# Two chained attentions on one core: held sums, halves added by ones products, a busy TensorE at the head

## The chip, the cores and the metric

The kernel runs on one core of a Trainium2 chip. The metric is the device time of one execution in microseconds (us). A core has TensorE for matrix products (PE in the profile; PEld is its weight load), VectorE (DVE), ScalarE (ACT), GpSimd (POOL) and SyncE (SP), which here issues transfers.

## The reference, cut to what matters

Eight images of 64 channels and 64 x 64 points (4096 tokens) pass two attention layers, all in fp32. Layer 0 has keys of 8 channels; layer 1 normalizes in groups first and has keys of 64 channels.

```python
# layer 0, per image
f = einsum('oc,bcn->bon', Wf, xf) + bf          # 8 x 4096
g = einsum('oc,bcn->bon', Wg, xf) + bg          # 8 x 4096
hh = einsum('oc,bcn->bon', Wh, xf) + bh         # 64 x 4096
beta = softmax(einsum('bci,bcj->bij', f, g), axis=2)
x = x + einsum('bcj,bij->bci', hh, beta)
# layer 1, per image
xn = group_norm(x, gamma, beta)                  # 8 groups of 8 channels
q, k, v = split(einsum('oc,bchw->bohw', w_qkv, xn) + b_qkv)
attn = softmax((q @ k) * 64**-0.5)
x = x + einsum('oc,bchw->bohw', w_proj, attn @ v) + b_proj
```

## The kernel before

An image's 4096 tokens lie in two halves of 64 partitions each. Each half of the queries is cut in four chunks of 512 columns (NC = 4, CW = 512), the keys in 16 tiles (NT = 16) of 2 x 128 tokens. Per tile TensorE makes scores, ScalarE makes their exponentials `e` (128 x 2048), TensorE weighs the values with them into an accumulator, and DVE adds the tile's exponentials into `esum`, from which the softmax denominators come. Six buffers hold exponentials: one is free again when it has been weighed and added.

The layers run in the order: layer 0 of image 0, layer 0 of image 1, layer 1 of image 0, layer 0 of image 2, layer 1 of image 1, and so on.

The adding, and the two ways by which a finished chunk gets its denominators:

```python
ppool = ctx.enter_context(tc.tile_pool(name="ppool", bufs=6))     # the exponentials "e"
...
at.weigh(acc, e[:, p], t, p, j == 0, j == 2 * NT - 1, cols)        # TensorE
...
added = vector.tensor_add(esum, first if t == 1 else esum, e).ins  # DVE, 128 x 2048
...
def halves():
    if other is not None:
        vector.tensor_add(raw, raw, other)
    vector.tensor_add(esum[:, 0], esum[:, 0], esum[:, 1])          # 128 x 1024

def transposed():            # one way: DVE adds over partitions by transposing, then 4 DMAs
    vector.tensor_reduce(part, esum[:, 0].rearrange("p h (i b) -> p b (h i)", b=32),
                         axis=AX.X, op=ALU.add, apply_transpose=True)
    ...
def sums(spare):             # the other: TensorE adds over partitions by products with ones
    for h in range(2):
        for i in range(2):
            row = 32 * (2 * h + i)
            matmul(z[row : row + 32, 0:width], ones[:, 0:32], esum[:, 0, h, ts(i, width)],
                   start=True, stop=True, tile_position=(0, row))
    nc.scalar.copy(zs, z[:, 0:width])
    ...                      # 4 DMAs to zt
def reciprocals(): ...       # reciprocal, one DMA out, two broadcasting DMAs back into r
def result():
    vector.tensor_mul(raw, raw, r)
    self.residual(raw, c)    # layer 0: raw + bias + x, and statistics for layer 1
```

Which way is taken, and when. A held chunk keeps its sums in a buffer that is free for the time, and its halves are added when layer 1 has begun:

```python
held = at.holds(c)
if at.kind == 1 or next_kind == 1 or held:
    when = now + 4
    if at.kind == 0:
        when = (i // NC + 1) * NC * NT + 1 + 3 * c       # in the layer 1 that follows
    for s, u in ((0, halves), (1, transposed), (5, reciprocals), (8, result)):
        at_step(when + s, behind(u), 0)
    return
behind(halves)()
at_step(now + delay, lambda: sums(spare), BANK)
at_step(now + delay + 4, behind(reciprocals), 0)
at_step(now + delay + 8, behind(result), 0)
...
def holds(self, c):
    return self.kind == 0 and self.b > 0 and c < (1 if self.b == 1 else NC - 1)
def home(self, c):                                        # where held sums lie
    if self.b > 1:
        if c == 0:
            layers1[self.b].own(F32)
        return layers1[self.b].parts[:, c, :]
    layers0[2].own_vt()
    return layers0[2].vt.rearrange("q p t c -> q (p t c)")
```

So all four chunks of image 0 and chunks 1 and 2 of image 1 go by `sums`, the others by `transposed`.

The start of image 0: the first 512 columns are projected straight to their places (`project_direct`), the rest by `project`, whose results are spread by DMAs. Both write to a buffer `full` of which there is one.

```python
def project_direct(self):
    full = work.tile([P, 2, CW], F32, tag="full", bufs=1, name="full_direct")
    high = work.tile([P, 2, CW], F32R, tag="high", bufs=1, name="high_direct")
    for i, dst in enumerate((self.f, self.g)):
        matmul(ps[:, i, :], direct[:, i, :], x_tiles[self.b][:, 0:CW], start=True, stop=True)
        nc.scalar.activation(full[:, i, :], ps[:, i, :], AF.Identity, bias=bias2[:, i : i + 1])
        vector.tensor_copy(high[:, i, :], full[:, i, :])
        vector.scalar_tensor_tensor(dst[:, 0:CW], high[:, i, :].bitcast(F32),
                                    lowmask2[:, i : i + 1], full[:, i, :], ...)
...
copy = vector.tensor_copy if self.kind == self.b == c == 0 else nc.scalar.copy   # values
...
for i in range(4):                                        # Newton steps for 1/sqrt(variance)
    vector.scalar_tensor_tensor(w, y, y, ve, op0=ALU.mult, op1=ALU.mult)
    vector.tensor_scalar(w, w, -0.5, 1.5, op0=ALU.mult, op1=ALU.add)
    vector.tensor_mul(y, y, w)
```

`matmul` and, where `tight` is set, `vector` keep their instructions in the order of the program; elsewhere a scheduler orders them.

Of the kernel before, what the change touches and what calls it, by code (L numbers as in the profile page):

```python
# [9 lines left out]
F32 = mybir.dt.float32  # L10
# [9 lines left out]
CW = 512  # L20
P = 128
# [47 lines left out]
def fast_path(  # L69
# [19 lines left out]
    nc = tc.nc  # L89
    B, C, N = x.shape  # L90
    C8 = WfT.shape[1]
    NH = N // 2
    NC = NH // CW
# [4 lines left out]
    const = ctx.enter_context(tc.tile_pool(name="const", bufs=1))  # L98
    xpool = ctx.enter_context(tc.tile_pool(name="xpool", bufs=3))
    proj = ctx.enter_context(tc.tile_pool(name="proj", bufs=1))  # L100
# [20 lines left out]

    made_last = {}
    added = None
    tight = False

    def in_order(made, engine="tensor"):

# [20 lines left out]
    vector = InOrder()  # L148

    def matmul(*args, **kwargs):  # L150
        in_order(nc.tensor.matmul(*args, **kwargs))  # L151

    def behind(work_):


        def made():
            with tc.issue_after(added):
                work_()

        return made  # L160
# [22 lines left out]
        return t  # L183


    w1 = const.tile([P, 2, C8], F32, name="w1")
    for i, (w, queue) in enumerate(((WfT, nc.scalar), (WgT, nc.sync))):
        for h in range(2):
# [24 lines left out]
    with tc.issue_after(masked):  # L213
# [10 lines left out]
        wfg = const.tile([P, 2, 4, C8], F32, name="wfg")  # L224
        nc.vector.tensor_copy(wfg, w1.unsqueeze(2).broadcast_to([P, 2, 4, C8]))
    wfg = wfg.rearrange("p i s c -> p (i s c)")
    fgb_low = const.tile([P, 2], F32, name="fgb_low")
    fgb, lowmask = fgb_low[:, 0:1], fgb_low[:, 1:2]
    for j in range(2):
# [20 lines left out]
    nc.vector.tensor_single_scalar(odd, lane, 1, op=ALU.bitwise_and)  # L250
    lowmask32 = const.tile([P, 1], F32, name="lowmask32")
    nc.vector.tensor_scalar(lowmask32, odd, -1.0, None, op0=ALU.mult)
    ones = const.tile([P, C], F32, name="ones")
    nc.vector.memset(ones, 1.0)


    QP = 2 * CW // P
# [67 lines left out]
    class Attention:  # L325
# [7 lines left out]

        def holds(self, c):

            return self.kind == 0 and self.b > 0 and c < (1 if self.b == 1 else NC - 1)

        def values(self, src, w, c):

            ps = pair()  # L340
            for t in range(TPC):
                for m in range(2):
                    for h in range(2):
                        matmul(
                            ps[ts(m, C), h, ts(t, C)], src[ts(h, C), ds(t * P + m * C, C)],
                            w[ts(h, C), :], start=True, stop=True,
                        )

            copy = vector.tensor_copy if self.kind == self.b == c == 0 else nc.scalar.copy
            copy(  # L350
                self.vt[:, :, ts(c, TPC), :],
                ps[:, :, 0 : TPC * C].rearrange("k p (t c) -> k p t c", c=C),
            )

        def finish(self, acc, esum, c, index):

            n = f"{self.name}_{c}"
            raw = work.tile([P, CW], F32, tag="raw", bufs=4, name=f"raw_{n}")
            other = self.total(raw, acc, index)
            zt = small.tile([P, QP], F32, tag="zt", bufs=4, name=f"zt_{n}")  # L360
            width = CW // 2
            r = four = None
# [4 lines that stand above are left out]
                vector.tensor_add(esum[:, 0], esum[:, 0], esum[:, 1])  # L367

            def transposed():


                nonlocal four
                both_ = work.tile([P, 8 * QP], F32, tag="zs", name=f"part_{n}")
                part = both_[:, 0:32]
                four = both_[:, 32:].rearrange("p (a k) -> p a k", k=QP)
                vector.tensor_reduce(
                    part, esum[:, 0].rearrange("p h (i b) -> p b (h i)", b=32),
                    axis=AX.X, op=ALU.add, apply_transpose=True,
                )
                for a in range(4):  # L380
                    nc.sync.dma_start(four[:, a, :], part[ts(a, 32), :])

            def sums(spare):

                z = banks[:, spare, :]

                zs = work.tile([P, width], F32, tag="zs", name=f"zs_{n}")
                for h in range(2):
                    for i in range(2):
                        row = 32 * (2 * h + i)  # L390
                        matmul(
                            z[row : row + 32, 0:width], ones[:, 0:32], esum[:, 0, h, ts(i, width)],
                            start=True, stop=True, tile_position=(0, row),
                        )
                nc.scalar.copy(zs, z[:, 0:width])
                for h in range(2):
                    for i in range(2):
                        row = 32 * (2 * h + i)
                        nc.sync.dma_start(zt[row : row + 32, :], zs[row : row + 1, :])  # L399

            def broadcast():
                nonlocal r
                r = work.tile([P, CW], F32, tag="r", name=f"r_{n}")

            def reciprocals():
                rt = stash[:, ts(index, QP)]
                if four is not None:
                    vector.tensor_reduce(
                        zt, four.rearrange("p a k -> p k a"), axis=AX.X, op=ALU.add
                    )  # L410
                vector.reciprocal(rt, zt)
                broadcast()
                dealt = recips[index]
                nc.sync.dma_start(dealt, rt)
                for h in range(2):
                    row = dealt[ts(h, C), :].rearrange("p e -> (p e)")
                    nc.sync.dma_start(r[ts(h, C), :], row.partition_broadcast(C))

            def result():
                vector.tensor_mul(raw, raw, r)  # L420
                self.residual(raw, c)

            return halves, transposed, sums, reciprocals, result
# [52 lines left out]
    class Layer0(Attention):  # L476
# [4 lines left out]
        def before(self):  # L481

            def begin():
                if self.b == 1:
                    self.own(F32R)
                else:
                    self.parts = proj.tile([P, 2, NH], F32R, tag="fg", name=f"fg_{self.name}")
                    if self.b != 2:  # L490
                        self.own_vt()
                self.f, self.g = self.parts[:, 0, :], self.parts[:, 1, :]
                self.st = small.tile(
                    [P, NC, nc.vector.BN_STATS_DIM], F32, tag="st", name=f"st_{self.name}"
                )
                if self.b > 0:
                    self.project_all()
                else:
                    self.project_direct()
                    self.project(0, (1,))  # L500

            def rest():
                self.project(1)
                with tc.issue_after(self.sent.ins):
                    for b in (1, 2):
                        load_x(b)

            if self.b == 0:
                return [(-1, begin, True), (0, rest, True)] + [
                    (  # L510
                        (-1, 1, 5, 8)[c],
                        lambda c=c: self.values(x_tiles[0][:, ts(c, CW)], wh, c),
                        True,
                    )
                    for c in range(NC)
                ]

            s, spread = (28, 32) if self.b == 1 else (0, 28)  # L520
            return [(s, begin, True), (spread, self.spread, False)] + [
                (
                    (36, 38, 43, 45)[c],
                    lambda c=c: self.values(x_tiles[self.b][:, ts(c, CW)], wh, c),
                    True,
                )
                for c in range(NC)
            ]
# [4 lines left out]
        def home(self, c):  # L533

            if self.b > 1:
                if c == 0:
                    layers1[self.b].own(F32)
                return layers1[self.b].parts[:, c, :]
            layers0[2].own_vt()
            return layers0[2].vt.rearrange("q p t c -> q (p t c)")  # L540

        def project_direct(self):

            ps = pair()
            full = work.tile([P, 2, CW], F32, tag="full", bufs=1, name="full_direct")
            high = work.tile([P, 2, CW], F32R, tag="high", bufs=1, name="high_direct")
            for i, dst in enumerate((self.f, self.g)):
                matmul(
# [110 lines left out]
    class Layer1(Attention):  # L659
# [8 lines left out]
        def before(self):  # L668
# [32 lines left out]
            def deviations():  # L701
# [8 lines left out]
                )  # L710
                y = guess.bitcast(F32)
                w = small.tile([P, 1], F32, tag="w", name=f"w_{n}")
                for i in range(4):
                    vector.scalar_tensor_tensor(w, y, y, ve, op0=ALU.mult, op1=ALU.mult)
                    vector.tensor_scalar(w, w, -0.5, 1.5, op0=ALU.mult, op1=ALU.add)
                    vector.tensor_mul(y, y, w)
# [179 lines left out]
    def finished(i, now):  # L896
# [7 lines left out]
        if at.kind == 1 or next_kind == 1 or held:  # L904
# [4 lines left out]
            for s, u in ((0, halves), (1, transposed), (5, reciprocals), (8, result)):  # L909
                at_step(when + s, behind(u), 0)  # L910
            return
        behind(halves)()

        spare = outer[c % 2 if at.kind == 0 else 1]
        delay = 7 if at.kind == 0 else 5
# [34 lines left out]
    i = 0  # L950
# [464 lines left out]
```

## Time and profile before

| | |
|---|---|
| time, median of three runs | 3005.96 us (3005.14 to 3006.3) |
| span of the profiled execution | 3004.0 us |
| busy: TensorE, DVE, ScalarE, GpSimd | 2973.7, 2574.0, 2073.0, 16.1 us |
| an addition of exponentials on DVE, 128 x 2048 | 2288 ns, 629 into `esum` from `esum` |
| adding two halves on DVE, 128 x 1024 | 1220 ns, 44 times |
| a transposing reduction on DVE, 128 x 1024 | 1967 ns, 38 times |
| first product on real data starts at | 7.26 us |
| first exponential of layer 1 starts at | 340.1 us |

Columns of the profile's rows: in a group of instructions, the line of the kernel, the engine, the operation, output<-input, then shapes, the count, and after the bar the busy time, the mean of one in ns and the idle time of the engine before it. A row of the timeline begins with start and duration in us, and ends in brackets with the idle time before it and what released it. Lines 141 and 151 are the helpers through which all ordered DVE and TensorE instructions go, so these are told apart by the names of their tiles.

### The profile page before, as it was taken

How to read it: one execution, taken by the hardware profiler on the slowest of the kernel's cores; microseconds unless marked ns; L12 is line 12 of the kernel's file. 1: busy time of each engine (PE TensorE's matmuls, PEld its weight loads, DVE VectorE, ACT ScalarE, POOL GpSimd, SP SyncE). 2: the span in 40 equal slices, each digit the busy share in tenths (PEclk: the TensorE clock that was granted, in tenths of full speed). 3: DMA queues.
4: the chain of work that ended last, by engine and by line, in shares of the span. 5: the costliest groups of instructions: out<-in, count | busy, mean ns of one | idle time of the engine just before them, and what ended most of it. 6: DMA issues, size and time to landing. Idle time of an engine off the chain costs nothing.

```text
span 3004.0 us, 58286 instructions
## 1 busy us (share of the span) xinstructions
PE 2973.7 (99%) x25629; PEld 1078.7 (36%) x25629; DVE 2574.0 (86%) x1659; ACT 2073.0 (69%) x2019; POOL 16.1 (1%) x40
## 2 busy tenths in 40 slices
PE   8999999999999999999999999999999999999998
PEld 3333333333333333333333333333333333333333
DVE  7999986899878998789986999879997799976776
ACT  6888656786567866678666785668856688566554
POOL 2000000000000000000000000000000000000000
PEclk9999999999999999999999999999999999999999
DMA  2100100101001010010100102000020000000000
GB/s 65 43 8 15 47 16 19 30 1 44 20 20 29 1 45 19 21 28 1 49 19 20 26 1 51 16 23 22 1 52 20 19 8 1 17 24 15 9 16 13
DMA packets 77141, 66.93 MB, mean 22 GB/s; under 512 B 54048, under 2 KB 54080, under 8 KB 75088
## 3 DMA queue, kind: packets, MB, share of 16 engines
q1 hardware_dynamic: 75792, 63.01, 8.7%
q8 instruction: 202, 3.31, 0.5%
q14 instruction: 59, 0.48, 0.1%
q0 software_dynamic: 768, 0.09, 0.0%
q10 hardware_dynamic: 320, 0.04, 0.0%
HBM read 39.84 MB, written 12.32 MB: 17 GB/s over the span
## 4 chain that ended last, share of the span: by engine, by line
PE 93%; DVE 4%; issue 1%; ACT 1%; DMA 0%; SPq 0%; DVEq 0%; ACTq 0%
PE banks L151 93%; DVE esum_l L141 3%; DVE vt_l L141 1%; ACT e_l L1013 1%; DMA x<-in_x_dram 0%; DVE x L141 0%; DVE raw_l L141 0%; DVE st_l L141 0%; ACT full_l L573 0%; DVE high_l L141 0%; DVE kq_l L141 0%; DVE rt L141 0%; SPq L399 0%; DMA zt_l<-zs_l 0%; DVE w_l L141 0%
## 5 line engine op out<-in xcount | busy, mean ns | idle before, releaser
L141 DVE TENSOR_TENSOR esum_l<-esum_l,e_l 128x2048 f32<-128x2048 f32 x629 | 1438.9, 2288 | 272.0 <-ACT e_l L972 246.3
L972 ACT ACTIVATE e_l<-banks 128x1024 f32<-128x1024 f32 x1024 | 992.2, 1022 | 680.6 <-PE banks L151 680.6
L151 PE MATMUL banks<-e_l,v_l 64*64 64x512 f32 (+1 forms) x8780 | 1090.2, 586 | 0.0
L1013 ACT ACTIVATE e_l<-banks 128x2048 f32<-128x2048 f32 (+3 forms) x727 | 953.8, 1373 | 183.5 <-PE banks L151 165.9
L151 PE MATMUL banks<-kq_l 64*64 64x512 f32 (+1 forms) x8448 | 1004.4, 585 | 6.5 <-ACT e_l L1013 5.7
L151 PE MATMUL banks<-e_l,vt_l 128*64 128x512 f32 (+1 forms) x4056 | 829.8, 550 | 0.0
L141 DVE TENSOR_TENSOR kq_l<-kq_l,e_l 128x2048 f32<-128x2048 f32 x252 | 577.5, 2292 | 24.4 <-ACT e_l L1013 0.5
L151 PEld LDWEIGHTS banks<-e_l,v_l 64*64 64x64 f32 (+1 forms) x8780 | 346.9, 133 | 589.3 <-issue 490.0
L151 PEld LDWEIGHTS banks<-kq_l 64*64 64x64 f32 (+1 forms) x8448 | 326.2, 134 | 602.9 <-issue 561.8
L151 PEld LDWEIGHTS banks<-e_l,vt_l 128*64 128x64 f32 x4056 | 267.8, 136 | 467.7 <-issue 447.6
L151 PE MATMUL banks<-fg_l 32*128 32x512 f32 x1792 | 204.7, 459 | 6.2 <-ACT e_l L1013 3.1
L141 DVE TENSOR_TENSOR esum_l<-e_l,e_l 128x2048 f32<-128x2048 f32 x45 | 102.3, 2274 | 86.2 <-ACT e_l L972 86.2
L151 PEld LDWEIGHTS banks<-fg_l 32*128 32x128 f32 x1792 | 84.8, 183 | 186.8 <-ACT e_l L1013 139.8
L141 DVE TRANSPOSE_TENSOR_REDUCE part_l<-esum_l 128x32 f32<-128x1024 f32 x38 | 74.7, 1967 | 0.0
L141 DVE TENSOR_TENSOR esum_l<-esum_l 128x1024 f32<-128x1024 f32 x44 | 53.7, 1220 | 0.4
L141 DVE TENSOR_TENSOR raw_l<-raw_l,r_l 128x512 f32<-128x512 f32 x63 | 43.2, 685 | 2.1 <-DMA r_l<-recips 2.1
L141 DVE TENSOR_TENSOR kq_l<-e_l,e_l 128x2048 f32<-128x2048 f32 x18 | 41.1, 2283 | 0.0
L651 ACT COPY raw_l<-banks 128x512 f32<-128x512 f32 x32 | 18.9, 590 | 25.2 <-PE banks L151 24.3
L141 DVE TRANSPOSE_TENSOR_REDUCE part_l<-kq_l 128x32 f32<-128x1024 f32 x18 | 35.2, 1955 | 0.0
L141 DVE TENSOR_TENSOR vt_l<-vt_l,e_l 128x2048 f32<-128x2048 f32 x14 | 32.1, 2291 | 1.2
L764 ACT ACTIVATE kq_l<-banks,kqb 64x256 f32<-64x256 f32 x64 | 30.1, 470 | 1.2
L151 PEld LDWEIGHTS banks<-wh,x 64*64 64x64 f32 x1024 | 21.2, 138 | 16.7 <-issue 15.8
(127 smaller groups left out, 467.9 us busy)
## 6 DMA issues: line engine op xcount, KB each, us to landing
r_l<-recips SPq DMA_DIRECT2D x126, 128.0 KB
kq_l<-kq_l SPq DMA_DIRECT2D x64, 128.0 KB
out_dram<-raw_l SPq DMA_DIRECT2D x62, 128.0 KB
x<-in_x_dram SPq DMA_DIRECT2D x30, 256.0 KB
fg_l<-fg_sent_l SPq DMA_DIRECT2D x24, 256.0 KB
fg_l<-fg_sent_l SPq DMA_DIRECT2D x48, 128.0 KB
part_l<-part_l SPq DMA_DIRECT2D x228, 4.0 KB
fg_sent_l<-high_l SPq DMA_DIRECT2D x28, 128.0 KB
```

What stands on the lines that cost most here:

```text
L141: it = getattr(nc.vector, name)(*args, **kwargs)
L151: in_order(nc.tensor.matmul(*args, **kwargs))
L651: nc.scalar.copy(raw, acc[0])
L764: nc.scalar.activation(self.q[ts(h, C), cols[1]], ps[other, 1, 0:width], AF.Identity, bias=k1["kqb"][other, :],)
L972: nc.scalar.activation(e[:, p], both_ps[p], AF.Exp, scale=at.scale)
L1013: nc.scalar.activation(e.rearrange("k p h n -> k (p h) n")[:, first_ : first_ + n_, :], banks[:, bank : bank + n_, :], AF.Exp, scale=at.scale,
```

## The change

It has seven parts. Chunks 1 and 2 of image 1 hold their sums for layer 1, in a new buffer `free` that takes the place of image 0's projections, which are no longer needed by then. Where sums go by ones products, both halves of `esum` are multiplied and added in the accumulator, and no halves are added on DVE. Products whose results nobody reads (18 on ones, 10 on the first weights) keep TensorE busy while the first loads are under way. The first values are copied by ScalarE. The second projection of image 0 is scheduled at step 2 in place of 0. `full_direct` lies in a buffer of the exponentials. The Newton steps are three in place of four, and DVE's order is kept from the beginning.

```diff
-    tight = False
+    tight = True
...
+    ones = const.tile([P, C], F32, name="ones")
+    nc.vector.memset(ones, 1.0)
+    def warm(rows, n):
+        for i in range(n):
+            matmul(banks[0:C, 7, 0:C], rows, rows, start=True, stop=True)
+    warm(ones, 18)
...
     wfg = wfg.rearrange("p i s c -> p (i s c)")
+    warm(wfg, 10)
...
-            return self.kind == 0 and self.b > 0 and c < (1 if self.b == 1 else NC - 1)
+            return self.kind == 0 and self.b > 0 and c < NC - 1
...
-            copy = vector.tensor_copy if self.kind == self.b == c == 0 else nc.scalar.copy
-            copy(
+            nc.scalar.copy(
...
-                for h in range(2):
-                    for i in range(2):
-                        row = 32 * (2 * h + i)
-                        matmul(
-                            z[row : row + 32, 0:width], ones[:, 0:32], esum[:, 0, h, ts(i, width)],
-                            start=True, stop=True, tile_position=(0, row),
-                        )
+                for p in range(2):
+                    for h in range(2):
+                        for i in range(2):
+                            row = 32 * (2 * h + i)
+                            matmul(
+                                z[row : row + 32, 0:width], ones[:, 0:32],
+                                esum[:, p, h, ts(i, width)],
+                                start=p == 0, stop=p == 1, tile_position=(0, row),
+                            )
...
-                return [(-1, begin, True), (0, rest, True)] + [
+                return [(-1, begin, True), (2, rest, True)] + [
...
-            layers0[2].own_vt()
-            return layers0[2].vt.rearrange("q p t c -> q (p t c)")
+            if c == 0:
+                layers0[2].own_vt()
+                return layers0[2].vt.rearrange("q p t c -> q (p t c)")
+            if c == 1:
+                self.free = proj.tile([P, 2, NH], F32, tag="fg", name="free")
+            return self.free[:, c - 1, :]
...
-            full = work.tile([P, 2, CW], F32, tag="full", bufs=1, name="full_direct")
+            full = ppool.tile([P, 2, 2, CW], F32, tag="e", name="full_direct")[:, 0]
...
-                for i in range(4):
+                for i in range(3):
...
-        behind(halves)()
```

More of the change, by code (lines that the diff above doesn't have):

```diff
@@ L252, in fast_path @@
     nc.vector.tensor_scalar(lowmask32, odd, -1.0, None, op0=ALU.mult)
-    ones = const.tile([P, C], F32, name="ones")
-    nc.vector.memset(ones, 1.0)
     QP = 2 * CW // P
```

## The prediction

> **What bounds the kernel now.** I read the shares of the engines and the chain first, then a table of stages, then the waits of ScalarE inside the one stage where TensorE idles, and last the first 28 us in order of time.
>
> ```profile
> PE 2973.7 (99%) x25629; PEld 1078.7 (36%) x25629; DVE 2574.0 (86%) x1659; ACT 2073.0 (69%) x2019; POOL 16.1 (1%) x40
> ...
> PE 93%; DVE 4%; issue 1%; ACT 1%; DMA 0%; SPq 0%; DVEq 0%; ACTq 0%
> ```
>
> TensorE is busy for 2973.7 of 3004.0 us. Whatever touches other engines can return at most the other 30.3 us, so the question is where these lie. The table of stages (columns: stretch, its length, then busy time of PE, PEld, DVE, ACT, POOL, the granted clock, the DMA share, GB/s):
>
> ```profile
> 7.00:25.05 18.05, 15.06 (x103) 5.62 (x103) 5.00 (x7) 7.72 (x7) 13.12 (x28) 0.72 0.27 65
> 28.30:105.00 76.70, 76.68 (x556) 28.91 (x556) 70.54 (x37) 64.67 (x63) 0.00 (x0) 1.00 0.29 72
> 105.00:315.00 210.00, 201.14 (x1370) 72.27 (x1361) 199.75 (x127) 168.96 (x147) 0.00 (x0) 1.00 0.05 14
> 315.00:340.00 25.00, 25.00 (x195) 9.25 (x195) 23.96 (x13) 17.94 (x19) 0.00 (x0) 1.00 0.04 12
> 340.00:563.00 223.00, 223.00 (x2322) 82.44 (x2312) 174.60 (x129) 136.07 (x155) 0.00 (x0) 1.00 0.12 28
> ```
>
> Three things are to be seen: TensorE waits 7.26 us for the first data and then runs at a reduced clock up to 25 us; it idles 8.86 us between 105 and 315 us, in layer 0 of images 0 and 1; from 315 us on it has no gap worth naming. In the stage with the idle time DVE is busy 95%. Back-to-back additions start 2.39 us apart and are counted 2.29 us each, so 95 to 96% is a full DVE. The waits of ScalarE there (name, then total us, times, longest) and its longest single one:
>
> ```profile
> ACT e_l L1013 <- DVE esum_l L141: 11.4, 12, 4.1
> ACT e_l L1013 <- DVE vt_l L141: 3.7, 3, 1.6
> ```
> ```profile
> 247.74 1.88 ACT L1013 ACTIVATE e_l<-banks 128x2048 f32<-128x2048 f32 x1 [4.09 <-DVE esum_l L141]
> ```
>
> An exponential cannot start because its buffer (six of them) is still to be added into the sums. TensorE then has no exponentials to weigh. The head, in order of time:
>
> ```profile
> 7.26 3.75 PE L151 MATMUL banks<-x,direct 128*128 128x512 f32 x4 [7.26 <-DMA x<-in_x_dram]
> ...
> 20.59 3.68 PE L151 MATMUL banks<-e_l,vt_l 128*64 128x512 f32 x8
> ...
> 25.33 1.94 PE L151 MATMUL banks<-e_l,vt_l 128*64 128x512 f32 x8
> ```
>
> The same eight matmuls take 3.68 us before 24 us and 1.94 us after 25 us. The granted clock is recorded as 0.50 from 15 to 25 us and 1.00 from 26 us.
>
> **What the Trainium skill says.** "TensorE: Matmul & The Clock Gate", Part 1: the array starts at half clock, goes to full after about 3.4 us of sustained activity in a free-running window, and falls back after an idle window. The trace agrees on the factor (3.68 against 1.94 us), and shows a fall at 15.0 us, after a gap of 1.6 us in which the products had ended. "VectorE: DVE Perf Modes", Mode 2x_2P: an fp32 tensor_tensor stays at one element a cycle; its table gives about 2293 ns for 2048 elements at that rate. The trace has 2288 ns: additions cannot be sped up, only left out. "TensorEngine Tiling (Array Packing)", Key Properties: a change of tiling mode drains the array. The ones products (four column tiles) take 0.57 us from their start at 75.61 to the next group's at 76.18; a pair of weighing records of 512 columns starts every 0.43 us, and the four ones products side by side stream two records of 256 columns each, one after the other, which is as long, so the change of mode costs about 0.14 us once per group, not per product.
>
> **The change part by part.**
>
> ```profile
> 63.13 1.23 DVE L141 TENSOR_TENSOR esum_l<-esum_l 128x1024 f32<-128x1024 f32 x1
> ...
> 75.61 0.64 PE L151 MATMUL banks<-esum_l,ones 128*32 128x256 f32 x8
> ```
>
> (a) *Halves by ones products.* Four chunks of image 0 each lose one half addition on DVE: 1.15 us to the next start (63.13 to 64.28). Each gets four more products on TensorE: 0.43 us, 1.7 us together, all on the bound engine.
>
> (b) *Image 1's sums held.* Chunks 1 and 2 lose their ones products: 2 x 0.57 = 1.1 us of TensorE. On DVE, two halves (2.3 us), a wait of 2.72 us for the sums' DMA at 283 us, and one residual (multiply, add, statistics: 297.59 to 299.70, 2.1 us) leave the layer 0 stage. In layer 1 of image 0 they come back with two transposing reductions of 1.9 us: about 8.6 us more there. In that layer DVE is busy 174.6 of 223 us, so it has room, though little in its first 50 us.
>
> (c) *One Newton step fewer.* Three small DVE operations, about 0.64 us (244.06 to 244.70), eight times. Only image 0's lies in the full stage; it falls just before the longest wait.
>
> (d) *Head.* Products on ones and wfg fill 1 to 7 us. If the clock is then full: the direct products shrink from 3.75 to about 1.9 us (1.9 saved); the first scores shrink by some 0.6; the second projection (1.98 us) and the first weighing (3.68 us) by half, 2.7. The copy of the first values leaves DVE, where it stood between a cast ending at 12.20 and the operation at 13.45 (1.25 saved), and full_direct has its own buffer, so the ScalarE wait that held the third score until 15.54 goes (0.6 saved). The second projection now comes behind the first two score groups, so it doesn't hold them. All added: 7.1 us at best by 25 us. The new order still has gaps between 10 and 14 us in which TensorE waits for ScalarE and DVE, like those before the fall at 15.0 us. I count 5 us.
>
> The sum needs DVE's position, not TensorE's alone. DVE catches up at 82 and 89 us, where it waits 1.33 us (sums' DMA) and 2.23 us (ScalarE): there it follows TensorE, so DVE's own earlier start is worth nothing more. At 89 us both are 5.0 - 0.4 (one ones group) = 4.6 us earlier. From there to 260 us DVE loses three halves and the Newton step: 3.45 + 0.64 = 4.1. TensorE gets three ones groups, 1.3 us. The idle time up to 260 us, 7.6 of the 8.86 us, falls by 5.4 to 2.2, and the end of that stretch comes 4.6 + 4.1 = 8.7 us earlier. Behind it DVE loses another 6 us or more, so the remaining 1.2 us of idle time goes, and 1.1 us of ones products: 11.0 us. From 340 us on TensorE has the same work. 3005.96 - 11.0 = 2995.0.
>
> **The rivals.** *DVE takes it all:* if the clock falls again at the head, only the removed waits count, 2.5 to 3 us there, and the rest as above: 8.5 to 9 us, 2997. For it: the fall at 15.0 us. Against: the order of the head looks tuned. *Nothing of the stage remains DVE-bound:* the full 8.86 us go, with 7 us at the head: 7 + 8.9 - 1.7 + 1.1 = 15.3, 2990.7. Against it is the wait of 4.09 us at 247, in front of which only 4.1 us of DVE work leaves. *The moved sums come back as a wait in layer 1:* DVE has 8.6 us more to do between 330 and 400 us, and transfers for two more chunks share the queue with image 2's projections, where a wait of 1.89 us for such a transfer already stands. If DVE falls some 14 us behind, the six buffers run out and TensorE stalls; I'd give that 2 to 4 us. Against it: DVE enters layer 1 about 5 us further ahead. *The warm-up products run past 7.26 us* and delay the first real ones, by 1 us or so.
>
> **Range and chances.** The head is worth 2.5 to 7 us, the idle time that remains 0 to 3, layer 1 may cost up to 3: 2990.5 to 3000. Two per cent would be 60 us, twice all idle time of TensorE, and nothing added is near that: faster 0.01, same 0.98, slower 0.01.
>
> **What would show it.** The direct products at 0.45 us or so each; full clock before 10 us and no fall; the exponential of 25.05 us near 20; DVE's first sum near 23.5 us instead of 27.28; idle TensorE between 95 and 305 us of 2 to 3 us; layer 1's first exponential near 329 us instead of 340.1; the stretch from there to the end unchanged at 2664 us. A TensorE gap in layer 1 of image 0, or a head that keeps its 0.50 clock, would make it wrong.

## The result

The changed kernel takes 2994.62 us (median of four runs, 2993.81 to 2995.09) against 3005.99 us for the kernel before (four runs, 3005.14 to 3006.3): ratio 0.9962, 95% interval 0.9945 to 0.998, so 11.4 us less, with an interval of 6 to 16.5 us. Two later measurements of the same kernel on other chips gave 2994.05 and 2994.37 us; over all its 14 runs the median is 2994.3.

The page of the changed kernel, engines and chain:

```profile
PE 2973.7 (99%) x25693; PEld 1082.2 (36%) x25693; DVE 2566.6 (86%) x1634; ACT 2072.6 (69%) x2019; POOL 15.9 (1%) x40
...
PE 98%; ACT 1%; DVE 1%; issue 0%; DMA 0%; SPq 0%; DVEq 0%; ACTq 0%
```

TensorE's busy time is the same to the last digit shown, 2973.7 us, in a span that is 11.1 us shorter (2992.9), but the two sums don't hold the same things. That of the changed kernel has 4.93 us of products that nobody reads, ahead of 7 us. Against them, the 103 records from the first product on real data to the third exponential are counted at 10.03 us in place of 15.06. So the head was won almost wholly by products that run faster, and what was won behind it (see the ledger) was idle time. DVE's share of the chain went from 4% to 1%. The table of stages, with the columns as before (the last row is layer 1 of image 0, which now begins 11.4 us earlier, hence its other window):

```profile
7.00:25.05 18.05, 14.77 (x128) 5.44 (x130) 8.38 (x9) 13.85 (x12) 12.88 (x28) 0.91 0.29 73
28.30:105.00 76.70, 76.69 (x569) 29.11 (x565) 70.05 (x36) 63.98 (x62) 0.00 (x0) 1.00 0.29 74
105.00:315.00 210.00, 207.17 (x1405) 74.49 (x1401) 201.99 (x120) 172.84 (x155) 0.00 (x0) 0.99 0.04 10
...
328.00:551.00 223.00, 223.00 (x2320) 82.44 (x2312) 180.63 (x136) 136.20 (x155) 0.00 (x0) 1.00 0.12 30
```

The granted clock of the head went from 0.72 to 0.91; it still isn't 1.00. Idle time of TensorE between 105 and 315 us went from 8.86 to 2.83 us. Layer 1 of image 0 took on 6 us of DVE work (174.6 to 180.6 us) without a gap on TensorE. ScalarE's waits for DVE between 95 and 305 us:

```profile
ACT e_l L1025 <- DVE free L141: 4.3, 3, 3.5
ACT e_l L1025 <- DVE esum_l L141: 0.6, 2, 0.4
ACT e_l L1025 <- DVE vt_l L141: 0.5, 1, 0.5
```

Where 11.4 and 3.7 us stood (between 28 and 330 us, a stretch for which the rows of the changed kernel are the same as these), 4.9 (`free` holds sums too, so its row counts with `esum`) and 0.5 remain, and 3.5 of it is one wait. TensorE at the head, in order of time:

```profile
7.25 1.95 PE L151 MATMUL banks<-x,direct 128*128 128x512 f32 x4 [0.86 <-DMA x<-in_x_dram]
...
16.75 2.28 PE L151 MATMUL banks<-e_l,vt_l 128*64 128x512 f32 x8
19.63 1.94 PE L151 MATMUL banks<-e_l,vt_l 128*64 128x512 f32 x8
```

The direct products took half the time (3.75 before). The first weighing took 2.28 us in place of 3.68, and the second projection just ahead of it 1.98 us as before: in this execution the granted clock fell to half at 14.0 us and came back at 17.5.

**The ledger.** Two events that both kernels have bound the stretches: ScalarE's third full exponential of image 0 (25.05 before, 19.52 after) and the first exponential of layer 1:

```profile
L984 ACT ACTIVATE e_l<-banks x1024: 1017/1023/1047, 328.7 to 2977.6; 128x1024 f32<-128x1024 f32 x171
```

328.7 in place of 340.1. Up to the third exponential 5.5 us were won; from there to layer 1 5.9 us (315.05 to 309.18); from there to the end nothing (2663.9 and 2664.2 us). For the middle stretch the sums of the stages of TensorE (and the other engines), first of the kernel before from 25.3 to 340.1 us, then of the changed one from 19.6 to 328.7 us:

```profile
sum 314.80, PE 305.32 PEld 111.11 DVE 297.28 ACT 254.67 POOL 0.00; mean PE 38.17 PEld 13.89 DVE 37.16 ACT 31.83 POOL 0.00
```
```profile
sum 309.10, PE 305.47 PEld 111.31 DVE 288.23 ACT 253.81 POOL 0.56; mean PE 38.18 PEld 13.91 DVE 36.03 ACT 31.73 POOL 0.07
```

TensorE's idle time in it fell from 9.48 to 3.63 us, 5.85 us, which is the whole 5.9; DVE has 9 us less to do there.

**What is left** is one place. TensorE from 236 us in the changed kernel:

```profile
236.61 2.37 PE L151 MATMUL banks<-e_l,v_l 128*64 128x512 f32 x12
240.18 0.51 PE L151 MATMUL banks<-kq_l 32*128 32x512 f32 x4 [1.21 <-ACT e_l L1025]
241.30 0.85 PE L151 MATMUL banks<-kq_l 32*128 32x512 f32 x2 [0.61 <-ACT e_l L1025]
242.64 0.70 PE L151 MATMUL banks<-kq_l 32*128 32x512 f32 x1 [0.49 <-ACT kq_l L777]
243.27 4.64 PE L151 MATMUL banks<-e_l,v_l 128*64 128x256 f32 x16
```

and ScalarE, for which they wait:

```profile
238.25 1.88 ACT L1025 ACTIVATE e_l<-banks 128x2048 f32<-128x2048 f32 x1 [3.45 <-DVE free L141]
```

It is the wait of 4.09 us at 247.74 in the kernel before, now 3.45 us. Its second cost is in the last row of TensorE: sixteen such products take 3.23 us elsewhere in both kernels and 4.64 us here. The granted clock is 0.50 from 242.8 to 246 us, behind a stretch of 3.4 us (239.4 to 242.8) in which TensorE was busy for only 1.52 us. The kernel before had the same pattern (1.54 us busy from 248.9 to 252.3), and in its one profile the clock didn't fall.

### The profile page after: what moved, and what is told of

Read it like the earlier page. It is cut to its first block, busy times and chain, and to the rows that moved or that the text cites. A ratio compares the mean times of both kernels' runs of the same rounds, so it can differ in the third digit from the quotient of the medians.

```text
span 2992.9 us, 58381 instructions
## 1 busy us (share of the span) xinstructions
PE 2973.7 (99%) x25693; PEld 1082.2 (36%) x25693; DVE 2566.6 (86%) x1634; ACT 2072.6 (69%) x2019; POOL 15.9 (1%) x40
## 4 chain that ended last, share of the span: by engine, by line
PE 98%; ACT 1%; DVE 1%; issue 0%; DMA 0%; SPq 0%; DVEq 0%; ACTq 0%
PE banks L151 98%; ACT e_l L1025 1%; DVE free L141 0%; DMA x<-in_x_dram 0%; ACT kq_l L777 0%; DVE rt L141 0%; DVE fg_l L141 0%; SPq L198 0%; DVE raw_end L141 0%; DVE w_l L141 0%; DVE guess_l L141 0%; DVE high_direct L141 0%; ACT kq_l L772 0%; ACT full_direct L564 0%; SPq L168 0%
## 5 line engine op out<-in xcount | busy, mean ns | idle before, releaser
L141 DVE TENSOR_TENSOR esum_l<-esum_l,e_l 128x2048 f32<-128x2048 f32 x601 | 1374.2, 2287 | 270.4 <-ACT e_l L984 248.5
L151 PEld LDWEIGHTS banks<-fg_l 32*128 32x128 f32 x1792 | 84.3, 182 | 183.4 <-ACT e_l L1025 140.6
L141 DVE TENSOR_TENSOR free<-free,e_l 128x2048 f32<-128x2048 f32 x28 | 64.2, 2291 | 2.6
L141 DVE TENSOR_TENSOR esum_l<-esum_l 128x1024 f32<-128x1024 f32 x38 | 46.3, 1219 | 0.2
```

The source lines that it names most:

```text
L141: it = getattr(nc.vector, name)(*args, **kwargs)
```

## The experiments

All are the changed kernel with one edit, except `head_only`, which is the kernel before with one part of the change, and `best`, which joins three edits. Kernels of one series ran on one chip, beside the kernel before; a difference from the changed kernel is the difference of the two gains over it. The changed kernel gains 10.6 us on each of the two chips of the experiments on which it ran. On the third, that of `head_only`, `newton8`, `fill` and `gps_mul`, it didn't run, and 10.6 us are assumed.

**The changed kernel again** (`after_again`, `after_third`), no edit.

> The changed kernel unaltered, as a yardstick on the same chip as the three runs beside it. Every theory: 2994.6 us, within 0.7 us of it.

> The changed kernel unaltered, beside the two runs above on the same chip: 2994.3 us within 0.7 us.

Measured: 2994.05 us (2991.53 to 2994.58), ratio 0.9961 (0.9948 to 0.9975), and 2994.37 us (2993.02 to 2995.03), ratio 0.9963 (0.9949 to 0.9976). In both profiles the clock of the head stayed full (1.00 in the stretch from 7 to 25.05 us), while in the first profile of this kernel it fell at 14.0 us. So the head differs from execution to execution. From the first product on real data to the third exponential it takes 10.77 us (6.86 to 17.63) and 10.78 us (6.51 to 17.29) in these two and 12.27 us in the first; the kernel before, profiled once, takes 17.79 us. The head without the fall of the clock thus gains 7.0 us, with it 5.5. `after_again`:

```profile
7.00:25.05 18.05, 15.07 (x155) 5.85 (x159) 8.72 (x10) 15.36 (x14) 12.56 (x26) 1.00 0.24 66
...
14.18 1.09 PE L151 MATMUL banks<-x,wfg 64*64 64x512 f32 x8
```

The fall behind the wait near 240 us was in all three, but not equally long: the sixteen products behind it take 4.64, 4.78 and, in `after_third`, 5.93 us.

```profile
242.27 5.93 PE L151 MATMUL banks<-e_l,v_l 128*64 128x256 f32 x16
```

From the third exponential to layer 1 the three profiles need 309.2, 309.8 and 311.6 us, so a difference of one or two microseconds between single profiles can come about without any edit.

**Without the products nobody reads** (`no_warm`).

```diff
-    warm(ones, 18)
...
-    warm(wfg, 10)
```

> The 28 products without a reader are left out; all else of the change stays. Theory (DVE waits for TensorE at 76 and 84 us, so whatever TensorE loses at the head is carried to the end): the direct products take 3.75 us again in place of 1.95 us, the first scores and values run at half clock, the third tile's exponential moves from 19.5 to about 22.7 us, and the time goes up by about 3 us to 2997.7 us. Rival 1 (DVE's full stage swallows the head's gain): within 1 us of 2994.6 us. Rival 2 (the clock falls again at 14 us anyway, so the products buy only the direct ones): 1.9 us, 2996.5 us.

Measured: 2995.95 us (2994.2 to 2997.79), ratio 0.9969 (0.9957 to 0.9981): 1.9 us more than the changed kernel on that chip. The direct products are slow again:

```profile
6.45 3.75 PE L151 MATMUL banks<-x,direct 128*128 128x512 f32 x4 [6.45 <-DMA x<-in_x_dram]
```

1.95 became 3.75 us; these 1.8 us match the difference of the medians. (In this profile `x` arrived 0.8 us earlier, as it does in some executions; the third exponential starts at 21.25 us, counted from the first product that is 2.5 us later than in the first profile of the changed kernel and 4.0 later than in `after_again`.) The clock from 7 to 25.05 us is 0.91 here too, as in the first profile of the changed kernel. So it is not the early products that keep the clock from lying at half up to 25 us, as it did in the profile of the kernel before; that leaves the other edits of the head. Which of them does it wasn't tested.

**The parts of the head alone, on the kernel before** (`head_only`): order kept from the beginning, early products, values copied by ScalarE, second projection at step 2, `full_direct` in its new buffer; sums, halves and Newton steps as before.

```diff
-    tight = False
+    tight = True
...
+    warm(ones, 18)
...
+    warm(wfg, 10)
...
-            copy = vector.tensor_copy if self.kind == self.b == c == 0 else nc.scalar.copy
+            copy = nc.scalar.copy
...
-                return [(-1, begin, True), (0, rest, True)] + [
+                return [(-1, begin, True), (2, rest, True)] + [
...
-            full = work.tile([P, 2, CW], F32, tag="full", bufs=1, name="full_direct")
+            full = ppool.tile([P, 2, 2, CW], F32, tag="e", name="full_direct")[:, 0]
```

> The kernel before with the head of the change alone: the products without a reader, first values by ScalarE, the second projection at step 2, a buffer of its own for full_direct, DVE's order kept. Halves, held sums and Newton steps are those of before. Theory: what the head gains by the third tile's exponential (25.05 to about 19 us, 5.5 to 6 us) is carried whole to the end, since DVE waits for TensorE's results between 80 and 90 us and is paced from there: 5 to 6 us under the kernel before, idle TensorE between 105 and 315 us still 8 to 9 us. Rival (DVE, full in that stage, swallows it): 2 to 4 us, and the idle time rises to 11 us or so.

Measured: 3000.55 us (2999.49 to 3003.06), ratio 0.9986 (0.9979 to 0.9993), 4.4 us less than before, where 5 to 6 were expected. Its stretch of 105 to 315 us:

```profile
105.00:315.00 210.00, 202.68 (x1330) 72.56 (x1332) 198.23 (x127) 168.77 (x150) 0.00 (x0) 0.98 0.05 11
```

7.32 us idle against 8.86: DVE's congestion hardly changes. The first exponential of layer 1 comes at 334.7 us, 5.4 us earlier than before. Here too sixteen products behind the wait near 240 us take 5.56 us in place of 3.23 us, 2.3 us that the kernel before doesn't pay in its profile. That is nearly all of what was lost on the way: the third exponential had started at 17.22 us, 7.8 us earlier than before.

**Halves added on DVE again** (`halves_dve`).

```diff
-                for p in range(2):
-                    for h in range(2):
-                        ...  # esum[:, p, h, ...], start=p == 0, stop=p == 1
+                for h in range(2):
+                    ...      # esum[:, 0, h, ...], start=True, stop=True
...
+        behind(halves)()
```

> Halves of image 0's four chunks are added by DVE again, with four ones products in place of eight per chunk. Theory (from 84 to 250 us DVE sets the pace): three halves of 1.15 us each lie in that stretch, 3.45 us more; one ones group fewer ahead of it, 0.4 us less; TensorE's other savings vanish in idle time. Time 2994.6 + 3.0 = 2997.6 us, idle TensorE between 105 and 315 us up from 2.8 to about 7.5 us. Rival (TensorE sets the pace throughout): 1.7 us of products fewer, 2992.9 us, idle time as in the changed kernel.

Measured: 2997.69 us (2996.4 to 2999.23), ratio 0.9975 (0.9966 to 0.9984), 3.6 us more than the changed kernel.

```profile
105.00:315.00 210.00, 203.85 (x1356) 72.84 (x1358) 202.03 (x121) 169.60 (x150) 0.00 (x0) 0.98 0.04 10
```

6.15 us of idle time in place of 2.83, and 0.9 us more between 28.3 and 105 us, where the changed kernel has none, though DVE is as busy (202.03 and 201.99 us): a full DVE shows the same share whether it is just keeping up or late, and only TensorE's idle time tells the two apart. ScalarE's waits for DVE are back: 3.7 us for buffers whose exponentials DVE still adds into the held sums in `vt` (0.5 in the changed kernel).

**Image 1's chunks 1 and 2 not held** (`not_held`).

```diff
-            return self.kind == 0 and self.b > 0 and c < NC - 1
+            return self.kind == 0 and self.b > 0 and c < (1 if self.b == 1 else NC - 1)
```

> Chunks 1 and 2 of image 1 go by ones products at once again, in place of being held for layer 1; these use the new eight products, so DVE gets no halves back, but the reciprocals, the wait for the sums' transfer and one residual. Theory: 2 x 1.0 us of ones products on TensorE, which is full there, plus some idle time of up to 1.2 us behind DVE: 2 to 3 us, 2996.6 to 2997.6 us. Rival 1 (moving the sums only shifts DVE work and layer 1 pays it back): within 1 us of 2994.6 us, and TensorE idle in layer 1 of image 0 in the changed kernel. Rival 2 (DVE is the bound there too): 5 us or more.

Measured: 2997.0 us (2994.78 to 2997.75), ratio 0.9972 (0.9961 to 0.9983), 2.9 us more. Its idle time up to 315 us is 3.37 us, 0.5 above 2.83. From the third exponential to layer 1 it takes 312.1 us (18.80 to 330.9), where `after_again` takes 309.8: 2.3 us. The two groups of ones products that come back are groups of sixteen records, 1.00 us each, so they make 2.0 us, and the idle time 0.5, together a little more than the 2.3. In the kernel before the two groups had eight records and took 0.57 us each, so this run costs more than the change had won by leaving them out. DVE's wait for the sums' DMA is back, as worked out. All such waits of the kernel:

```profile
DVE stash L141 <- DMA zt_l<-zs_l: 5.0, 2, 3.6
```

In the changed kernel this row is 1.5 us in one wait.

**Five Newton steps more per image** (`newton8`): eight in place of three, to enlarge a term too small to be measured.

```diff
-                for i in range(3):
+                for i in range(8):
```

> The changed kernel with eight Newton steps in place of three, so five more than it and more exact than either: 15 small DVE operations, 3.2 us, per image. Theory (a DVE operation ahead of the wait at 238 us costs its own length once, for image 0, and nothing for images 1 to 7, where DVE has room): 3.2 us slower than the changed kernel, some 2997.4 us, the wait for a free exponential's buffer up from 3.45 to about 6.6 us. Rival 1 (small operations hide): within 0.7 us. Rival 2 (they cost in every image): up to 25 us.

Measured: 2994.57 us (2994.42 to 2997.18), ratio 0.9967 (0.9954 to 0.9979): 0.2 us more than the changed kernel, where 3.2 were expected. The local effect is there in full:

```profile
240.03 1.88 ACT L1025 ACTIVATE e_l<-banks 128x2048 f32<-128x2048 f32 x1 [6.63 <-DVE free L141]
```

6.63 against 3.45 us, 3.2 us longer. But two smaller waits of TensorE behind it (1.21 and 0.61 us) are gone, merged into this one, and the idle time from 105 to 315 us is only 1.4 us longer (4.22). Its span is 1.2 us longer than that of `after_again` and 0.1 us shorter than that of `after_third`, whose heads were at full clock as well. So added DVE work at this place costs the path less than half of its length, and the medians cannot tell 0.2 from 1.4 us.

**More products nobody reads, between 9.8 and 13 us** (`fill`), to see whether the clock's fall in the head can be kept away.

```diff
+            if self.kind == self.b == 0 and c < 2:
+                warm(ones, (6, 8)[c])
             nc.scalar.copy(
```

> The changed kernel with 6 and 8 more products without a reader behind the first two groups of values, in the gaps of 0.95 and 1.3 us in which TensorE waits for ScalarE and DVE. Theory (those gaps let the clock fall at 14 to 17 us in some executions): no fall before 25 us in the profile, the second projection near 1.1 us in place of 1.7 to 2.0, the third exponential about 11 us after the arrival of x in place of 12.3; the time 0.5 to 1.5 us lower, 2993.3 us, and its scatter smaller. Rival (filling delays real work more than the clock gains): 0.5 us slower or more.

Measured: 2992.4 us (2992.29 to 2993.5), ratio 0.9959 (0.9946 to 0.9973), 1.9 us less than the changed kernel, a little more than expected, and with a scatter of 1.2 us where the changed kernel's runs lie 1.3 to 3.1 us apart. The head and its second projection:

```profile
7.00:25.05 18.05, 17.01 (x197) 7.84 (x197) 8.84 (x10) 15.82 (x14) 12.38 (x26) 1.00 0.25 67
```
```profile
13.73 1.09 PE L151 MATMUL banks<-x,wfg 64*64 64x512 f32 x8
```

Full clock, and the projection takes 1.09 us in place of the 1.98 of the first profile. The third exponential starts at 17.18 us, 10.78 us behind the first product (6.40). But `after_again` and `after_third` have the same 1.09 and 10.8 us without the filling. So the profile shows no gain over a head whose clock stayed. Nine profiles have this head without the filling, and in three of them the clock fell before 25 us (the first one of the changed kernel, `not_held` and `gps_mul`); it fell in neither of the two with the filling (`fill`, `best`). If the filling only prevents such falls of 1.5 us, a third of them is an estimated 0.5 us; where the rest of the 1.9 us comes from is not shown.

**The multiplication by the reciprocals given to GpSimd** (`gps_mul`), for image 0's four chunks, to relieve DVE by four operations of 0.7 us.

```diff
+            def multiplied():
+                nc.gpsimd.tensor_mul(raw, raw, r)
             def result():
-                vector.tensor_mul(raw, raw, r)
+                if not by_pool:              # by_pool: layer 0 of image 0
+                    vector.tensor_mul(raw, raw, r)
...
+        if at.kind == at.b == 0:
+            at_step(now + delay + 7, at.multiplied, 0)
```

> The changed kernel with the multiplication by the reciprocals of image 0's four layer 0 chunks done by GpSimd, which is idle then, in place of DVE: 0.72 us off DVE four times, all ahead of the wait at 238 us. Theory (DVE's work ahead of that wait is the pace): 2.9 us of DVE work less, idle TensorE between 105 and 315 us from 2.8 to 0.5 us or less, no fall of the clock at 244 us, which cost 1.4 us: 3 to 4 us faster, some 2990.8 us. Rival 1 (TensorE's own work is the bound by now): within 0.7 us of 2994.3 us. Rival 2 (DVE waits for GpSimd in its fixed order): slower.

Measured: 2994.38 us (2991.41 to 2996.44), ratio 0.9964 (0.9951 to 0.9978), no gain over the changed kernel. The first GpSimd multiplication ran while DVE was idle, the second beside DVE's additions:

```profile
81.23 1.28 POOL L431 TENSOR_TENSOR raw_l<-raw_l,r_l 128x512 f32<-128x512 f32 x1 [61.70 <-DMA r_l<-recips]
...
122.35 3.28 POOL L431 TENSOR_TENSOR raw_l<-raw_l,r_l 128x512 f32<-128x512 f32 x1 [39.85 <-DMA r_l<-recips]
```
```profile
117.41 12.76 DVE L141 TENSOR_TENSOR esum_l<-esum_l,e_l 128x2048 f32<-128x2048 f32 x5
```

Beside the second one, DVE's five additions take 12.76 us, where the same five take 11.88 us in the changed kernel: 0.88 us lost to save 0.7. The Trainium skill, "SBUF — State Buffer", section "SBUF: two separate sides", says that a DVE operation with two SBUF inputs and a GpSimd operation that reads SBUF exclude each other at a shared port pair, the later one waiting. The trace agrees that each delays the other (1.28 to 3.28 us, 11.88 to 12.76 us). At the third, DVE also waits 1.17 us for GpSimd. Behind the fourth it is 0.6 us ahead of the changed kernel (209.27 against 209.89 us at the same operation), no more than it was at the head (0.7), so DVE was not relieved, and this run doesn't test what relief is worth.

**Statistics and first projections of layer 1 later** (`late_stats`). Ahead of the wait near 240 us, DVE does 18 operations between 230 and 240 us, most of them small ones of image 0's statistics. If it only had to catch up on these, moving them behind should remove the wait.

```diff
-            at = [18, 23, 26] if self.b == 0 else [20, 25, 27]
+            at = [18, 31, 33] if self.b == 0 else [20, 25, 27]
...
-                s = 31 + 8 * c if self.b == 0 else 35 + 7 * c
+                s = 38 + 8 * c if self.b == 0 else 35 + 7 * c
```

> The changed kernel with image 0's layer 1 statistics, normalizing and projections scheduled 7 to 8 steps (some 18 us) later; no operation is added or left out. Theory A (DVE's work summed up to 238 us sets the wait there, so taking the statistics' 4.3 us of small operations out of that stretch lets DVE catch up in the stretch behind it, where no residuals are left): the wait of 3.45 us and the clock's fall behind it go, idle TensorE between 105 and 315 us under 1 us, 3 to 4.5 us faster, some 2990.5 us. Theory B (the wait is that of the chain statistics, normalizing, projection itself, wherever it stands, as the eight Newton steps' 3.7 us wait for it suggests): the wait moves to about 255 us and the time stays within 1 us.

Measured: 2994.11 us (2992.43 to 2996.75), ratio 0.9964 (0.9951 to 0.9978), no difference from the changed kernel. The wait moved along with the statistics and kept its size:

```profile
253.52 1.88 ACT L1025 ACTIVATE e_l<-banks 128x2048 f32<-128x2048 f32 x1 [3.40 <-DVE free L141]
```

My reading that another place would spare it falls. From 230 to 240 us DVE is busy 9.34 us with the small operations in that window and 9.58 us with additions in their place: at neither place do they find slack, and the six buffers run out behind them by the same amount.

**The best of these together** (`best`): the edits of `fill` and `late_stats`, and each Newton step in two operations in place of three.

```diff
+                vector.tensor_scalar(ve, ve, -0.5, None, op0=ALU.mult)
                 for i in range(3):
-                    vector.scalar_tensor_tensor(w, y, y, ve, op0=ALU.mult, op1=ALU.mult)
-                    vector.tensor_scalar(w, w, -0.5, 1.5, op0=ALU.mult, op1=ALU.add)
-                    vector.tensor_mul(y, y, w)
+                    vector.scalar_tensor_tensor(w, y, ve, y, op0=ALU.mult, op1=ALU.mult)
+                    vector.scalar_tensor_tensor(y, w, 1.5, y, op0=ALU.add, op1=ALU.mult)
```

> late_stats, with the filled gaps at the head and a Newton step of two DVE operations in place of three. If both theories behind them hold: 2992.4 - 3 to 4.5 = about 2988.5 us. If the wait only moves: 2992 us.

Measured: 2991.26 us (2991.07 to 2993.18), ratio 0.9955 (0.9941 to 0.9969): 13.7 us less than before and 3.1 us less than the changed kernel on the same chip. `fill` alone had 1.9 us on another chip; that the rest is more than scatter is not shown, and the span of the profile, 2991.3 us, is that of `after_again` (2991.4). A seventh buffer of exponentials, the plainest way to the wait that is left, wasn't tried.

## Why the prediction was right, by its steps

2995.0 us was predicted. The sum was -11.0 us, and -11.4 was measured. That it came so close is partly luck, since errors of opposite sign cancel. In the profiles, 5.1 us were won by 89 us (4.6 worked out), 2.8 from there to the end of the stretch near 250 us (4.1), and 3.5 behind it (2.3).

The runs taken apart give 4.4 us for the head (`head_only`), 3.6 for the halves (`halves_dve`) and 2.9 for the held sums (`not_held`), 10.9 together, against the 10.6 of the changed kernel. This is weak support: the interval of `head_only` alone reaches from 2.1 to 6.3 us, and 2.0 of the 2.9 us of `not_held` are groups of ones products which took 1.1 us in the kernel before. What the parts do is better read from the traces: the head makes products faster, the halves take idle time from TensorE, and of the held sums it is mostly the ones products left out that count. None of them uncovers a new bound.

- *The bound.* Right for what the change could reach: the idle time that went lay ahead of 315 us, DVE made that of the stage, and from layer 1's first exponential on nothing changed (2664 us, as predicted; that exponential at 328.7 us, predicted 329). Not all of the 30.3 us of idle time lay ahead, though: 10.8 us lie behind 315 us, 8.4 of them in the last 24 us, and they stayed.
- *Head, 5.0 us.* 5.5 by the third exponential (19.52; "near 20" predicted), 4.4 as a part alone. DVE's first sum starts at 22.84 us (23.5 predicted). Wrong in its detail: I asked for "full clock before 10 us and no fall", and in the first profile the clock did fall at 14.0 us, for 3.5 us, after a stretch with gaps of about 1 us each. The time came out well because 5 us had been counted where 7.1 were possible. The two profiles without the fall show 7.0, so "near 20" holds only with the fall that the prediction had named as a sign of being wrong. Within the head only the early products were tested alone.
- *Early products.* Mis-sized in what was asked of `no_warm`: 3 us expected, 1.9 found, which is about the direct products' 1.8 us. Its ranges and those of the changed kernel overlap, and its profile is 2.5 us later at the third exponential, so the exact size is open.
- *Halves, 3.45 us off DVE against 1.7 us on TensorE.* The products cost what was worked out: a ones group with its return to the other tile shape takes 1.00 us (70.08 to 71.08), 0.43 more than 0.57. The net was larger than the difference of the two for the whole kernel, 3.6 us and not 3.45 - 1.7: `halves_dve` brings back 3.3 us of idle time in the stage and 0.9 us ahead of 105 us, which my sum had not counted, 4.2 us against the 1.7 of the products. That makes 2.5 us; the other 1.1 us I can't place. Its clock between 240 and 250 us is 0.70 in place of 0.83, but `after_third`, with no edit, has 0.66.
- *DVE follows TensorE at 82 and 89 us, and its own earlier start is worth nothing more.* Both waits stayed, moved along to 76.7 and 84.2 us, with 1.48 and 2.64 us in place of 1.33 and 2.23. Right.
- *Idle time of the stage, 8.86 us down to about 2.2, all of it ahead of 260 us.* 2.83 us are left, all at one place. Two terms failed. The Newton step was counted in full (0.64 us); `newton8` puts five such steps at 0.2 to 1.4 us and not 3.2, so its part of my sum was at most 0.3, if a step left out counts like one added. And the clock's fall behind the wait was not foreseen: 4.64 - 3.23 = 1.4 us lost there. The stretch that ends with these products was left 7.9 us earlier (255.78 to 247.91) and not 8.7 as worked out. From 89 us on 2.8 us were won and not 4.1, and the clock's 1.4 us alone are as much, so the first profile leaves the Newton step's share open.
- *Behind that, 1.2 us of idle time and 1.1 us of ones products.* 3.5 us were found (84.3 to 80.8 us). Idle time went from 1.25 us to almost nothing and the two ones groups left, as predicted; the same 124 score products are counted at 15.7 us in place of 17.0, with no wait among them, which is the rest. Why they are shorter was not tested.
- *The rivals.* Moved sums as a wait in layer 1: no, 223.00 of 223 us busy, with 6.0 us more for DVE where 8.6 had been counted. The whole stage freed of DVE: no, one wait stayed, at the place named against it. A head with no clock gain: no, though its own evidence, the fall of the clock, did come back in part. Early products that delay the first real ones: not in the first profile, where TensorE waited 0.86 us for `x` behind them; in `after_again` and `after_third` it went from them to the real ones without a wait (6.86 and 6.51 us), so a delay of some tenths isn't excluded there.

The cause of the remaining wait is only bounded: it is a free buffer that is waited for, it moves with the statistics (`late_stats`), it grows with work put there (`newton8`), and its size hardly answers to the place. How much DVE work must leave to end it stays open.

## What to carry to other kernels

When one engine is full over a stage and another waits for it, read the second one's idle time, not the first one's share: 202 us of DVE went with 2.83 and with 6.15 us of idle time. Here work paid when it left the full engine for one that has gaps at that point, even though that is the bound of the whole kernel (3.6 us for the halves). Moved to a stage with room, it returned 0.5 us of idle time; moved within the stage (`late_stats`), nothing. Where a start at half clock costs time, products without a reader are a cheap filler: 28 of them ahead of the data were worth 1.9 us. Fourteen more in the gaps behind brought the median down by another 1.9 us, though the profile shows no faster head than the unfilled one at its best. And look at several profiles of one kernel before a stretch of a few microseconds is explained.

## What the runs showed of the hardware

The Trainium skill, "TensorE: Matmul & The Clock Gate", Part 1, speaks of a fall of the clock after an idle window. Here windows that were partly busy were enough: 1.27 us busy in 3.4 ahead of the fall at 14.0 us, 1.52 in 3.4 ahead of that at 242.8 us. Each of these two lasted about 3.4 us; that of `after_third` lasted 6.7 us (241.0 to 247.6), and that of the kernel before at the head 10 us (15.0 to 25.2). The kernel before, with 1.54 in 3.4 us, had no fall there, nor had the head of `after_third`, with 1.23 in 3.4 us ahead of 13.4. So the same gaps bring a fall in one execution and none in another. The page's free-running window could explain that (gaps cut by a window's edge count less), but no run here isolates it.

A GpSimd multiplication of 128 x 512 elements in fp32 took 1.28 us alone and 3.28 us beside DVE's additions, which lost 0.88 us themselves.
